# Splitting the scalings of int4 weight granules into parts behind named ScalarE copies

## The chip, the cores and the metric

The program runs on one core of one Trainium2 chip. The profile names the core's engines: PE (TensorE, matmuls; PEld is its weight load), DVE (VectorE), ACT (ScalarE), POOL (GpSimd) and SP (SyncE, which here issues nearly all DMAs). Each engine runs its own instructions in the order in which the program lists them and waits on semaphores for the others. The metric is device time in microseconds, lower is better; the kernel before takes 1338.17 us (median of three runs, 1336.70 to 1338.47).

## The reference

A block of 2048 tokens of width 1024 is normalised; the output is the input plus two branches on the normalised rows: a long convolution along the width with a kernel of a state-space model (S4), and a gated feed-forward layer whose weights are int4 with a scale and a zero for each group of 64.

```python
def dequantize(W_q, scale, zero):
    hi = W_q >> 4 & 15
    lo = W_q & 15
    w = jnp.stack([hi, lo], axis=-1).reshape(out, half * 2)
    w = (w.reshape(out, -1, 64) - zero[:, :, None]) * scale[:, :, None]
    return w.reshape(out, half * 2)
...
xn = layernorm(x)                                  # x: 1 x 2048 x 1024
g = einsum('bsh,ih->bsi', xn, Wg)                  # Wg, Wu: 2752 x 1024
u = einsum('bsh,ih->bsi', xn, Wu)
y = einsum('bsi,hi->bsh', silu(g) * u, Wd)         # Wd: 1024 x 2752
out = x + s4_convolution(xn) + y
```

## The kernel before

**Numbers and products.** Values are kept as pairs of f16 (a high and a low part), and a product takes three matmuls: high by high, high by low, low by high (PASS). Gate and up, and later down, are multiplied by a Strassen-like scheme of seven products in place of eight (PROD, line 63): sums of the token blocks (made by combine, lines 237 to 285) are multiplied by sums of the weight blocks (made by sums, lines 336 to 345).

**Granules.** Weights come in granules of 128 x 1024. j counts 21 column blocks of gate and up; granules 2j and 2j + 1 belong to block j. A granule of gate/up is made so, all in one buffer w:

- load_raw: the raw int4 words and the scales and zeros, two loads issued by SP (lines 292 to 298);
- unpack: two DVE instructions, w <- raw (lines 309, 310);
- scale_c: three small POOL instructions that turn scale and zero into a factor and an offset, sz <- sz (lines 320 to 325);
- w_scale: 16 ACT instructions, one for each group of 64, w <- w,sz (lines 327 to 334);
- w_sums: four DVE instructions, w <- w;
- w_hi: two ACT casts, nat <- w; w_lo: two DVE subtractions, nat <- w,nat; w_t: two transposing DMAs on SP, wf <- nat.

The pools in the gate/up stage: one buffer w, five of "nat" (shared with the down weights' nd and with the work tiles of S4), four raw, two sz, four wf (two blocks' worth). wf of block j + 1 takes the place of block j - 1.

**Order of the stages.** First the 16 norms of 128 rows each (norm_stat, norm_hi, norm_lo: DVE, POOL, ACT, DVE), blocks j = 0 and 1 in plain products (gate_up_plain), combine(0) and combine(1) for the two halves cp of the tokens, and granules 4 to 7. The norms and combines on DVE and ACT are chained in program order (pin). Then the gate/up stage: 38 units gate_up(j, cp), with the down weights (load_wd, four steps a unit from j = 4 on) and the S4 kernel's preparation (s4) as steps between them. Then the convolution, and the down product.

**A unit** (gate_up, lines 595 to 648) is seven products of 12 matmuls. Its ACT work is six instructions: the copy of A to B, of C to hb, of B to D, the Silu of A, and, for the last unit's pending products 4 and 3, the copy of C to ha and the Silu of D. Product 6 adds into B and product 5 into D, so PE needs those two copies.

**What sets the order.** The program is written as a sequence of instructions for each engine by a planner: it takes an instruction when its inputs and its buffer are free by the planner's own time model, and among those that are ready the one that stands first in the text. tc.issue_after(x) adds that what is traced under it and runs on the engine of x stands behind x on that engine; it is a lower bound and no wait. Under heads[behind] all 16 scalings of the granules 2j + 2 and 2j + 3 stand behind the copy of B in unit (j - 1, 1) (lines 384 to 386 and 991 to 994), and their text stands ahead of the units of j. BEHIND = {4: 13} puts the unpack of granule 4 (and, as tiles of one name are handed out in the order of the text, the granules after it) behind the subtraction of norm 13. FETCH traces the loads of granules 8 and 9 under an instruction of POOL; they are SP's, so it moves nothing.

```python
for j in range(2, NJ):
    if 3 <= j < NJ - 1:
        load_w(2 * j + 2, (j - 1, 1))
        load_w(2 * j + 3, (j - 1, 1))
    for cp in range(2):
        if cp or j > 3:
            gate_up(j, cp, wt[j])
```

The last two granules (G_WP, the rest of the down weights) are made after the units of j = 19.

Of the kernel before, what the change touches and what calls it, by code (L numbers as in the profile page):

```python
# [24 lines left out]
F16 = mybir.dt.float16  # L25
# [3 lines left out]
AF = mybir.ActivationFunctionType  # L29
# [4 lines left out]
P = 128  # L34
# [4 lines left out]
NJ = 21  # L39
# [3 lines left out]
G_WP = G_WD + 2 * NPAIR  # L43
# [4 lines left out]

SPG = 8
FETCH = {8: 15, 9: 15}  # L50
BEHIND = {4: 13}

XS = 64.0
WS = 1024.0
# [33 lines left out]
def build(nc, tc, x, xp, raw_d, sz_d, par_d, vct_d, tab_d, csrow_d, out):  # L88
# [3 lines left out]
    with es:  # L92
# [12 lines left out]
        WPN = dr.tile([P, 2, 2048], F16, name="WPN")  # L105
# [8 lines left out]
        V, A = Engine(tc, nc.vector), Engine(tc, nc.scalar)  # L114
        SP, G, PE = Engine(tc, nc.sync), nc.gpsimd, Engine(tc, nc.tensor)
# [22 lines left out]
        def wtemp(kind, shape, dtype, name):  # L138
            return home[kind].tile(shape, dtype, tag=kind, name=name, **({"bufs": szbufs[0]} if kind == "sz" else {}))
# [35 lines left out]
        rs, los = {}, {}  # L175
# [110 lines left out]


        with ea:
            slots, heads, tails, ends = {}, {}, [], [None]
            rawt = {}  # L290

            def load_raw(gi):
                raw = wtemp("raw", [P, 16, 32], I32, f"raw{gi}")
                ld = SP
                ld.dma_start(raw, raw_d[gi].rearrange("p (a b) -> p a b", a=16))
                sz = wtemp("sz", [P, 2, 16], F32, f"sz{gi}")
                ld.dma_start(sz, sz_d[gi])
                return raw, sz
# [21 lines left out]
            def scale_c(gi, sz):  # L320

                G.tensor_scalar(sz[:, 0], sz[:, 0], WS, None, ALU.mult)  # L322
                G.tensor_tensor(sz[:, 1], sz[:, 1], sz[:, 0], ALU.mult)
                G.tensor_scalar(sz[:, 1], sz[:, 1], -1.0, None, ALU.mult)
                return sz

            def scale_a(w, sc, groups=range(16)):

                wv = w.rearrange("p a b -> p (a b)")
                for g in groups:  # L330
                    A.activation(
                        wv[:, 64 * g : 64 * g + 64], wv[:, 64 * g : 64 * g + 64].bitcast(I32), AF.Identity,
                        bias=sc[:, 1, g : g + 1], scale=sc[:, 0, g : g + 1],
                    )
# [30 lines left out]
            def wtile(gi):  # L365
                if gi not in wft:
                    wft[gi] = wfp.tile([P, 28, P], F16, tag="wf", name=f"wf{gi}")
                return wft[gi]
# [9 lines left out]
            made, halved = {}, {}  # L378

            def w_unpack(gi):  # L380
                w, sz = unpack(gi)
                made[gi] = w, scale_c(gi, sz)

            def w_scale(gi, part, behind=None):
                with tc.issue_after(heads[behind].ins) if behind in heads else nullcontext():
                    scale_a(*made[gi], range((0, 5, 11)[part], (5, 11, 16)[part]))

            def w_sums(gi):
                sums(made[gi][0], False)
# [8 lines left out]
            def w_lo(gi):  # L398
                w, _ = made.pop(gi)
                for k, nat in enumerate(halved[gi]):  # L400
                    V.tensor_tensor(nat[:, :, 1], w[:, :, P * k : P * k + P], nat[:, :, 0], ALU.subtract)

            def w_t(gi):
                wf = wtile(gi)
                for k, nat in enumerate(halved.pop(gi)):
                    last[0] = SP.dma_start_transpose(wf[:, 14 * k : 14 * k + 14], nat.rearrange("p a b c -> p (a b c)"))
                wt.setdefault(gi // 2, []).append(wf)

            def load_w(gi, behind=None):
                if gi in BEHIND:  # L410
                    with tc.issue_after(los[BEHIND[gi]].ins):
                        w, sz = unpack(gi)
                    made[gi] = w, scale_c(gi, sz)
                else:
                    w_unpack(gi)
                for part in range(3):
                    w_scale(gi, part, behind)
                w_sums(gi)
                w_hi(gi)
                w_lo(gi)  # L420
                w_t(gi)


            def wp_hi(i):
                made[G_WP + i] = made[G_WP + i][0], wtemp("nat", [P, 1024], F16, f"wph{i}")
                w, hi = made[G_WP + i]
                A.copy(hi, w.rearrange("p a b -> p (a b)")[:, :1024])

            def wp_lo(i):
                w, hi = made.pop(G_WP + i)  # L430
                lo = wtemp("nat", [P, 1024], F16, f"wpl{i}")
                V.tensor_tensor(lo, w.rearrange("p a b -> p (a b)")[:, :1024], hi, ALU.subtract)
                SP.dma_start(WPN[:, i, 0:1024], hi)
                SP.dma_start(WPN[:, i, 1024:2048], lo)

            def scales_t():

# [154 lines left out]

            pending = []

            def gate_up(j, cp, wf):

                def prod(i, ps, start, stop):
                    fa, fb = PROD[i]
                    xt = xtile(cp, fb)
                    for kt in range(4):  # L600
                        for n, (wi, xi) in enumerate(PASS):
                            ends[0] = PE.matmul(
                                ps, wf[kt // 2][:, 14 * (kt % 2) + 2 * fa + wi, :], xt[:, xi, kt, :],
                                start=(start and kt == 0 and n == 0), stop=(stop and kt == 3 and n == 2),
                                skip_group_check=not start,
                            )

                def rest(i):
                    if len(pending) > i:
                        pending[i]()  # L610

                nm = f"{j}_{cp}"
                isc = 1.0 / (XS * WS)
                add, mult = ALU.add, ALU.mult
                bA, bB = bank("A" + nm), bank("B" + nm, "B")
                prod(1, bA, True, True)
                heads[j, cp] = A.copy(bB, bA)
                bC = bank("C" + nm)
                prod(7, bC, True, True)
                tag = "h" if j % 2 else "e"  # L620
                hb = htile("hb_" + nm, tag)
                A.copy(hb, bC)
                rest(0)
                prod(6, bB, False, True)
                bD = bank("D" + nm, "D")
                A.copy(bD, bB)
                rest(1)
                pending.clear()
                prod(2, bA, False, True)
                A.activation(bA, bA, AF.Silu, scale=isc)  # L630
                prod(5, bD, False, True)
                tails.append(V.tensor_tensor(hb, bD, hb, add))

                def fourth():
                    prod(4, bC, False, True)
                    ha = htile("ha_" + nm, tag)
                    A.copy(ha, bC)
                    V.tensor_tensor(ha, bB, ha, add)
                    V.scalar_tensor_tensor(ha, ha, HS * isc, bA, mult, mult)
                    pending[1] = lambda: third(ha)  # L640

                def third(ha):
                    prod(3, bD, False, True)
                    A.activation(bD, bD, AF.Silu, scale=isc)
                    V.scalar_tensor_tensor(hb, hb, HS * isc, bD, mult, mult)
                    finish_h(j, cp, ha, hb)

                pending.extend((fourth, None))
# [283 lines left out]
            wt = {j: [wtile(2 * j), wtile(2 * j + 1)] for j in range(2)}  # L932
# [53 lines left out]
            wd_steps = (None for u in range(NPAIR) for _ in load_wd(u))  # L986
            s4_steps = s4()

            gate_up(2, 0, wt[2])
            gate_up(3, 0, wt[3])  # L990
            for j in range(2, NJ):
                if 3 <= j < NJ - 1:
                    load_w(2 * j + 2, (j - 1, 1))
                    load_w(2 * j + 3, (j - 1, 1))
                for cp in range(2):
                    if cp or j > 3:
                        gate_up(j, cp, wt[j])
                    for _ in range(4 if j >= WD_FROM else 0):
                        next(wd_steps, 0)
                    for _ in range(3 - cp if j >= S4_FROM else 0):  # L1000
                        next(s4_steps, 0)
                if j == NJ - 2:
                    for i in range(2):
                        w_unpack(G_WP + i)
                        for part in range(3):
                            w_scale(G_WP + i, part)
                        wp_hi(i)
                        wp_lo(i)
            settle()
            for steps in (wd_steps, s4_steps):  # L1010
                for _ in steps:
# [163 lines left out]
        for cp in range(2):  # L1175
# [12 lines left out]
            behind = []  # L1188
# [216 lines left out]
```

## Time and profile before

| | us |
|---|---|
| median of three runs | 1338.17 |
| the profiled execution | 1336.8 |
| its span (first to last instruction) | 1335.0 |
| norms, plain products, combine(0) | 0 to about 133 |
| gate/up stage | about 133 to 884 |
| convolution, then the down product | 884 to 1335 |
| PE idle from 133 to 150 | 7.5 |
| PE idle from 150 to 350 | 0.05 |
| PE idle from 350 to 884 | 30.2 |

A line of the timeline gives start, length, engine, source line, operation and, in brackets, how long the engine had been idle and what ended that. L77 is the line in which the helper class records an instruction, L82 the same for those chained by pin, so tiles tell the lines apart: w<-w,sz are scalings, nat<-w the casts of gate/up granules, nd<-w those of the down weights. The granted clock of PE has two values in this profile, full and half.

### The profile page before, as it was taken

The numbers are of one execution on the slowest core, as the hardware profiler recorded it, in microseconds if no ns is written. First come the engines' busy times: TensorE is split into PE (matmuls) and PEld (weight loads), VectorE is DVE, ScalarE is ACT, GpSimd is POOL, SyncE is SP. The second block draws the span as 40 slices with busy tenths as digits, with TensorE's granted clock in tenths as the row PEclk, the third lists the DMA queues.
The fourth block names the chain that finished last, engine by engine and source line by source line (L and its number), as shares of the span: only waits on it lengthen the run. The fifth ranks groups of instructions, "written<-read, shape, count | busy, mean of one in ns | idle before, by whom it ended". The sixth has DMA issues, their size and how long they took to land. (4 is left out here: it accounts for less than half of the span.)

```text
span 1335.0 us, 20888 instructions
## 1 busy us (share of the span) xinstructions
PE 1277.1 (96%) x7880; PEld 751.0 (56%) x7880; DVE 991.1 (74%) x1344; ACT 669.1 (50%) x1208; POOL 189.7 (14%) x267
## 2 busy tenths in 40 slices
PE   6999799999999989989989999999999999999998
PEld 5644344444444434434433444456557888888887
DVE  7759986568797787779668687662738897779792
ACT  4777457647664745557466756720204433443330
POOL 3220010100000100111001001000000022255540
PEclk8999899999999998999999999999999999999999
DMA  6792947459896988699789979695937779799991
GB/s 224 181 189 52 218 137 137 124 142 234 193 257 160 236 204 226 156 226 239 185 222 226 242 191 223 201 281 183 329 132 296 259 201 270 241 260 265 288 189 50
DMA packets 358400, 276.02 MB, mean 207 GB/s; under 512 B 211668, under 2 KB 304668, under 8 KB 354204
## 3 DMA queue, kind: packets, MB, share of 16 engines
q1 hardware_dynamic: 335676, 261.59, 71.4%
q0 software_dynamic: 21760, 10.49, 6.6%
q10 hardware_dynamic: 864, 2.62, 0.6%
q8 instruction: 61, 1.00, 0.3%
q14 instruction: 39, 0.32, 0.1%
HBM read 132.36 MB, written 94.84 MB: 170 GB/s over the span
## 5 line engine op out<-in xcount | busy, mean ns | idle before, releaser
L77 PEld LDWEIGHTS <-wf 128*128 128x128 f16 x3960 | 374.1, 99 | 473.7 <-issue 40.6
L77 PEld LDWEIGHTS <-g 128*128 128x128 f16 x2940 | 287.6, 98 | 33.5 <-issue 0.2
L77 ACT ACTIVATE w<-w,sz 128x64 f32<-128x64 int32 x640 | 217.1, 426 | 64.1 <-DVE w L77 54.4
L77 PE MATMUL A<-x,wf 128*128 128x512 f16 x912 | 216.7, 384 | 13.9 <-DMA wf<-nat 13.1
L77 PE MATMUL D<-x,wf 128*128 128x512 f16 x912 | 214.3, 382 | 10.3 <-ACT D L77 9.7
L77 PE MATMUL C<-x,wf 128*128 128x512 f16 x912 | 210.2, 381 | 1.2 <-ACT hb L77 1.2
L77 DVE TENSOR_TENSOR w<-w 128x256 f32<-128x256 f32 (+2 forms) x272 | 139.0, 527 | 77.6 <-ACT w L77 71.3
L77 ACT CAST g<-a 128x2560 f16<-128x2560 f32 x42 | 97.5, 2324 | 180.8 <-PE cv L77 51.2
L77 PE MATMUL A<-b,g 128*128 128x256 f16 x1680 | 185.9, 273 | 0.0
L77 DVE TENSOR_TENSOR g<-a,g 128x2560 f16<-128x2560 f32 x42 | 118.3, 2819 | 30.9 <-ACT g L77 30.9
L1257 POOL DMA_DIRECT2D out<-o x64 | 78.7, 2105 | 342.7 <-DVE o L77 334.2
L322 POOL TENSOR_SCALAR sz<-sz 128x16 f32<-128x16 f32 x42 | 29.6, 705 | 685.3 <-DMA sz<-in_sz 588.5
L77 PE MATMUL B<-x,wf 128*128 128x512 f16 x456 | 108.1, 388 | 9.6 <-ACT B L77 9.5
L77 ACT CAST nd<-w 128x896 f16<-128x896 f32 x70 | 63.5, 933 | 67.0 <-DVE w L77 56.0
L77 PE MATMUL D<-b,g 128*128 128x256 f16 x840 | 94.0, 273 | 0.0
L77 ACT CAST nat<-w 128x896 f16<-128x896 f32 x76 | 68.1, 936 | 46.0 <-issue 31.2
L77 DVE TENSOR_TENSOR nd<-w,nd 128x896 f16<-128x896 f32 x70 | 75.2, 1082 | 21.4 <-ACT nd L77 21.3
L77 DVE TENSOR_TENSOR nat<-w,nat 128x896 f16<-128x896 f32 x76 | 80.2, 1085 | 13.9 <-ACT nat L77 13.8
L77 PEld LDWEIGHTS <-x 128*128 128x128 f16 x576 | 52.4, 98 | 23.8 <-issue 2.7
L77 DVE SCALAR_TENSOR_TENSOR p<-cv,p 128x512 f32<-128x512 f32 x32 | 21.9, 686 | 49.5 <-PE cv L77 47.7
L77 PE MATMUL cv<-band,x 128*128 128x512 f16 (+3 forms) x384 | 57.0, 299 | 0.0
L77 PE MATMUL g<-x,wf 128*128 128x128 f16 (+1 forms) x336 | 48.5, 292 | 1.5 <-ACT wf L82 0.8
(145 smaller groups left out, 1199.6 us busy)
## 6 DMA issues: line engine op xcount, KB each, us to landing
a<-HF SPq DMA_DIRECT2D x28, 1280.0 KB, 8.0
WD<-nd SPq DMA_DIRECT2D x70, 448.0 KB, 4.2
b<-WD SPq DMA_DIRECT2D x49, 640.0 KB, 6.0
w<-SZT SPq DMA_DIRECT2D x80, 256.0 KB, 5.5
raw<-in_raw SPq DMA_DIRECT2D x65, 256.0 KB, 3.5
HF<-ha SPq DMA_DIRECT2D x54, 256.0 KB, 3.3
HF<-s SPq DMA_DIRECT2D x40, 256.0 KB, 3.5
HF<-hb SPq DMA_DIRECT2D x36, 256.0 KB, 3.1
```

The costliest lines, as they stand in the source:

```text
L77: return method(*args, **kw)
L322: G.tensor_scalar(sz[:, 0], sz[:, 0], WS, None, ALU.mult)
L1257: G.dma_start(dst, o[:, q], accum_op=ALU.add)
```

## The change

- The granules from 8 on, and the two of G_WP, are made by one generator, w_flow, that the units drive. It does one granule in a unit's time: behind the copy of B to D 8 scalings; behind the Silu of A the other 8, then the loads of the next granule are traced and the sums; behind the next unit's copy of A to B the two casts, and then the subtractions, the transposes and the unpack of the next granule. The ties are again issue_after, so lower bounds.
- The flow begins in the second unit (3, 0). Granule g is scaled in unit number g - 7 (the first unit is 0) and cast at the head of the next one.
- The text of the parts stands right behind the copy that they are tied to, no longer ahead of both units of j.
- Granule 4's unpack stands behind the subtraction of norm 15 instead of 13, and its three POOL instructions behind POOL's last one of norm 15.
- wp_hi and wp_lo do the same as before with another index.

```diff
-BEHIND = {4: 13}
+BEHIND = {4: 15}
...
-            def w_scale(gi, part, behind=None):
-                with tc.issue_after(heads[behind].ins) if behind in heads else nullcontext():
-                    scale_a(*made[gi], range((0, 5, 11)[part], (5, 11, 16)[part]))
+            def w_scale(gi, groups=range(16)):
+                scale_a(*made[gi], groups)
...
-            def load_w(gi, behind=None):
+            def load_w(gi):
                 if gi in BEHIND:
                     with tc.issue_after(los[BEHIND[gi]].ins):
                         w, sz = unpack(gi)
-                    made[gi] = w, scale_c(gi, sz)
+                    with tc.issue_after(rs[15, 0].ins):
+                        made[gi] = w, scale_c(gi, sz)
...
+            def w_flow():
+                order = list(range(8, 2 * NJ)) + [G_WP, G_WP + 1]
+                for n, gi in enumerate(order):
+                    w_unpack(gi)
+                    for groups in (range(8), range(8, 16)):
+                        mark = yield
+                        with tc.issue_after(mark.ins):
+                            w_scale(gi, groups)
+                    if n + 1 < len(order):
+                        rawt[order[n + 1]] = load_raw(order[n + 1])
+                    if gi < G_WP:
+                        w_sums(gi)
+                    mark = yield
+                    with tc.issue_after(mark.ins):
+                        (w_hi if gi < G_WP else wp_hi)(gi)
+                    if gi < G_WP:
+                        w_lo(gi)
+                        w_t(gi)
+                    else:
+                        wp_lo(gi)
+                while True:
+                    yield
...
-                heads[j, cp] = A.copy(bB, bA)
+                seed = A.copy(bB, bA)
+                if len(started) > 1:
+                    side.send(seed)
...
-                A.copy(bD, bB)
+                seed = A.copy(bD, bB)
+                if len(started) == 1:
+                    next(side)
+                if started:
+                    side.send(seed)
...
-                A.activation(bA, bA, AF.Silu, scale=isc)
+                seed = A.activation(bA, bA, AF.Silu, scale=isc)
+                if started:
+                    side.send(seed)
+                started.append((j, cp))
...
-                if 3 <= j < NJ - 1:
-                    load_w(2 * j + 2, (j - 1, 1))
-                    load_w(2 * j + 3, (j - 1, 1))
...
-                if j == NJ - 2:
-                    for i in range(2):
-                        w_unpack(G_WP + i)
-                        for part in range(3):
-                            w_scale(G_WP + i, part)
-                        wp_hi(i)
-                        wp_lo(i)
```

## The prediction

> **What bounds the kernel now.** I read the page first, then the windows by stage, the waits of TensorE (PE) inside the gate/up stage, and the timeline at its longest idle times. The page's first line and the group of scalings:
>
> ```profile
> PE 1277.1 (96%) x7880; PEld 751.0 (56%) x7880; DVE 991.1 (74%) x1344; ACT 669.1 (50%) x1208; POOL 189.7 (14%) x267
> ...
> L77 ACT ACTIVATE w<-w,sz 128x64 f32<-128x64 int32 x640 | 217.1, 426 | 64.1 <-DVE w L77 54.4
> ```
>
> PE is busy for 96% of the span: all the change can win is PE idle time and half-clock time. By windows:
>
> ```profile
> 133.00:150.00 17.00, 9.46 (x24) 2.43 (x23) 16.97 (x23) 9.65 (x17) 0.00 (x0) 0.70 1.09 196
> 150.00:350.00 200.00, 199.95 (x938) 91.16 (x937) 141.34 (x228) 118.83 (x259) 14.32 (x36) 1.00 0.69 167
> ```
>
> (Columns: window, length, busy time and count of PE, PEld, DVE, ACT, POOL, granted clock, DMA share, GB/s.) PE starves at 133-150, where DVE has no idle time left; it never waits at 150-350; the rest of its waits lie at 350-884. Waits of PE from 133 to 884 us (engine and tile waited for, us in total, times, longest):
>
> ```profile
> PE A L77 <- DMA wf<-nat: 13.1, 12, 3.3
> PE D L77 <- ACT D L77: 9.7, 7, 4.1
> PE B L77 <- ACT B L77: 9.5, 4, 3.4
> ```
>
> One of the waits for a ScalarE (ACT) copy, in the timeline of all engines:
>
> ```profile
> 672.26 5.41 ACT L77 ACTIVATE w<-w,sz 128x64 f32<-128x64 int32 x16 [2.91 <-DVE w L77]
> ...
> 677.57 0.57 ACT L77 COPY B<-A 128x512 f32<-128x512 f32 x1
> ...
> 678.20 1.02 PE L77 MATMUL B<-x,wf 128*128 128x512 f16 x4 [3.42 <-ACT B L77]
> ```
>
> All 16 scalings of a granule stand as one block before the copy of A to B, and PE waits 3.42 us for it.
>
> **Part 1: half bursts behind named copies.** A block of 16 takes 5.41 us (0.34 each). One unit is 84 matmuls of 0.216 us, 18.1 us. Between the end of product 1 and the start of product 6, which needs the copy of B, lie products 7 and the last unit's 4: 2 x 12 x 0.216 = 5.2 us, less the copy's 0.57: 4.6 us of slack. D's copy has the same slack before product 5. A block of 5.41 exceeds it; the new half of 8 (2.7 us) doesn't, nor do the two casts (1.78 us). And a half stands right behind D's copy or the Silu of A, so the next urgent copy is a product or more away. Gaps that I put to a 16-block in the ACT timeline: 0.69 us (at 358), 1.24 + 0.58 (562), 2.82 (578), 3.42 (678), 2.71 (794), 0.56 (840): 12.0 us. Two of them were followed by a half-clock stretch of 3.4 us, 1.7 us lost each. Together 15.4. The bounds: 0 if all are replaced, 15.4 if all go; I take **-12**, near the upper end, since the slack covers the halves but other ACT work (casts for the down weights, 0.93 us each) still comes between.
>
> The clock is weighed here. Rows: after PE idled 2.71 us at 794.69, twelve matmuls took 4.44 us instead of 2.75; after 2.82 us at 578.66 they took 2.75. The Trainium skill (TensorE: Matmul & The Clock Gate, section "Why this matters for your kernels") asks for no PE-idle gaps over some 3 us; by it the 2.71 us gap would have cost no clock and the upper end would be 13.7, not 15.4. The rows decide: a gap just under 3 us can cost clock.
>
> **Part 2: odd granules earlier.** PE waits for turned weights (wf) at 482-730: 1.00, 0.92, 0.99, 0.76, 0.73, 0.64, 0.52, together 5.6 us. All are a unit's first product waiting for the second granule of its pair, whose casts started 1.6 to 11.3 us after the B copy of the unit before (at 563.8 against 552.5, for one). They are now traced behind that copy. Worked out from a unit's start: B copy ends at 3.2, casts at 5.0, landing 7 to 8 us later (casts ended 721.4, landed 729.6): 13.2 us, against 18.1 when it is needed, 4.9 us spare. The sums before the casts (4 x 0.42 on DVE) wait for the second half behind Silu A: 15.6 + 0.6 + 2.7 = 18.9, so 20.6, which is 2.5 us into the next unit, before the B copy. Bounds: -5.6 (all gone) to +5 (the new order is late by 0.3 us in each of 17 iterations); I take **-3**.
>
> **Part 3: granule 4 behind the last norm.** In the timeline at 87-104:
>
> ```profile
> 87.69 5.41 ACT L77 ACTIVATE w<-w,sz 128x64 f32<-128x64 int32 x16
> ...
> 94.93 1.23 ACT L82 ACTIVATE n<-n,rs 128x1024 f32<-128x1024 f32 x1
> ...
> 96.06 4.07 ACT L77 ACTIVATE w<-w,sz 128x64 f32<-128x64 int32 x12
> ...
> 100.80 1.05 ACT L82 CAST n<-n 128x1024 f16<-128x1024 f32 x1
> ...
> 101.87 1.22 DVE L82 TENSOR_TENSOR n<-n 128x1024 f16<-128x1024 f32 x1 [0.38 <-ACT n L82]
> ```
>
> The scalings of granules 4 and 5 stand before the last norm (its Pool step ended at 90.33). DVE idles 2.52 + 0.90 + 3.59 + 0.88 + 0.38 = 8.3 us there, and every later step of combine(0) stands behind the row at 101.87. With granule 4's unpack behind that row, ACT does 1.23 + 1.05 after 90.33 and the row starts near 92.7, 9.2 us earlier; DVE is saturated afterwards, so combine(0) ends up to 8.3 us sooner. At 133-150 PE did 24 matmuls, 5.2 us of work in 17: 11.8 lost. What is late next: the second operand of product 7, from combine(0)'s end, and granule 5's halves. The latter's transposes were issued at 134.8 though they were ready at 124.4, because SP stood behind a store at 126.1-130.9; 8 us of delay there costs nothing. Bounds: +2 (the weights become the last) to -8.3; I take **-6**, near the DVE rows. Pool's three instructions for granule 4 (0.26, 1.10, 0.25 at 30.6-32.4) now stand behind norm 15's, done by 91.9, before the unpack ends: 0. The Pool wait at 64.6-69.5 is for granule 7's scales, which the change doesn't tie: 0.
>
> **Part 4: everything that moves along.** Per granule: a raw and a scale load (SP, 0.38 and 0.33 us issue), two unpacks on DVE (0.42), three Pool steps, 16 scalings, 4 sums, 2 casts, 2 subtractions (1.08), 2 transposes on SP. Counts stay. Granule 9's loads are traced twice (once as prefetch, once by FETCH): 272 KB, some 0.7 us of SP, at 190-210 where PE doesn't wait: 0; without that cover 3.5 us, the landing time of a raw load. The halves now wait for the unpack right behind D's copy; behind them on ACT stand the Silu of the last unit's D and of A, for which only products on DVE and a bank needed a unit later wait: 0. The casts behind the B copy are different: if one waits for a "nat" buffer, the copies hb, ha and D stand behind it, and PE waits for D. That happened before:
>
> ```profile
> 498.17 1.78 ACT L77 CAST nd<-w 128x896 f16<-128x896 f32 x2 [9.11 <-issue]
> ...
> 502.00 0.59 ACT L77 COPY D<-B 128x512 f32<-128x512 f32 x1
> ...
> 502.64 1.01 PE L77 MATMUL D<-x,wf 128*128 128x512 f16 x2 [4.11 <-ACT D L77]
> ```
>
> Gaps of this kind: 0.42, 1.36, 0.77, 4.11, 0.58, 1.77 = 9.0 us, and 2.9 of half clock after 4.11: 12 us, 2.0 each. No buffer is added, and an even granule's pair is held longer (casts 3 us into a unit, but its wf slot is free only after the pending product 3, 13 us into it). Bounds: -6 (half of them go, since the copies stand first) to +56 (34 units at 2.0, less the 12 there are); I take **+2**, nearest to the six rows.
>
> **Sum.** The profiled execution took 1336.8 us (span 1335.0 and 1.8 around it): 1336.8 - 12 - 3 - 6 + 2 = 1317.8. The median of the three runs, 1338.17, is 1.4 above it: **1319 us**.
>
> **Rivals.**
> 1. *Only the blocks go or only the norms move*: the order is laid out by a planner on its own estimates, so one of parts 1 and 3 may not take effect (the norms' cast may be put behind other ACT work; the blocks may join again, since a tie is only a lower bound). 1338.2 - 6 to -12 with the +2 kept and part 2 gone: about 1328 to 1334. For: ACT waits 51.9 us for DVE before scalings, so halves may bunch. Against: the D copy now stands between.
> 2. *Slower, by nat buffers*: casts right behind each B copy meet full buffers. Price 2.0 us per unit; it cancels the 21 us of parts 1 to 3 from 10 to 11 units on. In 24 of 34 units: 1338.2 + 48 - 12 - 21 = 1353. For: five buffers, two held 15 us or more per even granule, and the s4 tables take up to three. Against: 150-350 shows no PE wait at the same pace.
> 3. *All goes well*: 15.4 + 5.6 + 8.3 + 6 = 35 us less: 1303.
>
> **Chances.** Forecast (1308 to 1327) 0.42, rival 1 (1328 to 1341) 0.22, rival 2 0.24, rival 3 0.12. A measurement here can tell 0.2% (2.7 us) from no change. Faster 0.67 (forecast, rival 3 and 0.13 of rival 1), same 0.08, slower 0.25 (the rest of rival 1 and rival 2). The range 1303 to 1350 leaves out 0.19: the far part of rival 2 (0.14) and 0.05 of rival 3. The likeliest case's own range is 1308 to 1327.
>
> **What would show it.** Right: no block of 16 scalings on ACT in the gate/up stage; waits of PE for ACT's B copies near 0 instead of 9.5 us; the last norm's subtraction near 93 instead of 101.87; PE idle at 133-150 under 3 us. Wrong: ACT casts "nat" waiting several us behind a B copy with "PE D <- ACT D" growing; new PE waits for wf at unit starts; granule 4's weights landing after 140.

## The result, and the profile after

The changed kernel takes 1343.68 us (median of six runs, 1341.27 to 1347.04) against 1336.88 us (six runs, 1332.38 to 1338.47) for the kernel before: a ratio of 1.0062, 95% interval 1.0049 to 1.0075. It is slower by 0.6%, where the forecast said 1319 us and faster. The profiled execution took 1347.04 us, the longest of the six, and its span is 1343.6.

The same views as for the kernel before, now of the changed one. The page: the sum of PE's work is nearly the same, and a group that had waited for little now has 53.4 us of idle time of VectorE before it (columns: busy us, mean ns, idle before and what ended most of it).

```profile
PE 1280.8 (95%) x7880; PEld 751.1 (56%) x7880; DVE 992.1 (74%) x1344; ACT 671.1 (50%) x1208; POOL 188.2 (14%) x267
...
L77 DVE TENSOR_TENSOR w<-raw,w 128x1024 f32<-128x1024 int16 x20 | 24.4, 1220 | 53.4 <-DMA raw<-qn 53.4
```

The windows, the last one the whole gate/up stage (133 to 884 before, where PE was busy for 713.22 of 751 us):

```profile
133.00:150.00 17.00, 12.06 (x48) 4.30 (x47) 16.91 (x24) 10.45 (x23) 0.00 (x0) 0.90 1.03 183
150.00:350.00 200.00, 197.41 (x923) 89.05 (x922) 135.41 (x222) 116.74 (x258) 13.55 (x34) 1.00 0.70 169
133.00:893.00 760.00, 717.26 (x3279) 318.49 (x3278) 562.48 (x922) 452.36 (x975) 57.70 (x108) 0.98 0.83 199
```

PE did 48 matmuls in 133 to 150 where it had done 24, but the stage ends 10 us later. PE's waits from 133 to 893 us:

```profile
PE A L77 <- DMA wf<-nat: 33.7, 25, 3.2
PE D L77 <- DVE hb L77: 3.1, 2, 2.0
PE B L77 <- ACT B L77: 2.2, 2, 1.6
PE C L77 <- DVE ha L77: 1.4, 1, 1.4
PE D L77 <- ACT D L77: 1.3, 2, 1.0
```

The waits for ScalarE's copies of B and D fell from 19.2 us to 3.5, as meant. In their place PE waits for turned weights: 28.8 of the 33.7 us lie after 160 us, at the first product of units (j, 0), where the kernel before had 5.6. The half-clock time from 150 to 900 us also rose, from 17.1 to 23.9 us; from 133 us on it is 27.3 us in both, since the kernel before had 10.2 us of it in the first 17 us.

Where it was lost: I compared the time at which PE reaches the matmuls of the n-th unit in both traces. The changed kernel is 3.1 us ahead half a unit in and 0.8 at unit 4, 0.7 behind at unit 13, 10.2 behind at unit 16, then between 1.3 and 10.8 behind, and 10.1 at the end of the stage. After the stage the difference no longer grows: the two profiled executions differ by 10.2 us (the medians by 6.8).

Two stretches of the timeline show how a granule comes late. First, the odd granule 17 in the changed kernel. The copy that its casts are tied to started at 348.12, and its four sums had ended by 351.2:

```profile
354.24 0.94 ACT L77 CAST nd<-w 128x896 f16<-128x896 f32 x1 [3.50 <-DVE w L77]
...
358.04 0.94 ACT L77 CAST nd<-w 128x896 f16<-128x896 f32 x1 [2.38 <-DVE w L77]
358.88 1.77 ACT L77 CAST nat<-w 128x896 f16<-128x896 f32 x2
...
361.19 5.07 SPq L77 DMA_TRANSPOSE wf<-nat  x2
...
363.03 1.09 DVE L77 TENSOR_TENSOR nat<-w,nat 128x896 f16<-128x896 f32 x1
...
366.55 0.82 PE L77 MATMUL A<-x,wf 128*128 128x512 f16 x3 [1.98 <-DMA wf<-nat]
```

The casts (nat) were ready at 351.2 and ran at 358.88, because two casts for the down weights (nd) stood ahead of them in ScalarE's order and those waited for VectorE. The second subtraction, the second transpose and PE followed late in turn. Second, granule 19:

```profile
396.74 1.26 SPq L77 DMA_TRANSPOSE raw<-qn  x1
...
403.87 1.23 DVE L77 TENSOR_TENSOR w<-raw,w 128x1024 f32<-128x1024 int16 x1 [4.97 <-DMA raw<-qn]
...
406.12 1.78 ACT L77 CAST nat<-w 128x896 f16<-128x896 f32 x2 [6.44 <-DVE w L77]
...
408.82 3.70 SPq L77 DMA_TRANSPOSE wf<-nat  x2
...
412.98 0.82 PE L77 MATMUL A<-x,wf 128*128 128x512 f16 x3 [1.98 <-DMA wf<-nat]
```

Here VectorE itself stands: at the first instruction of a down granule's dequantisation, for a transpose of its raw words that was issued late. The last sums of granule 19 and the rest stand behind it. VectorE's waits, of the changed kernel from 150 to 900 us and then of the kernel before from 150 to 884:

```profile
DVE w L77 <- DMA raw<-qn: 53.4, 10, 9.0
```

```profile
DVE w L77 <- DMA w<-SZT: 29.2, 14, 5.7
```

So VectorE stood there before too, for the table of scales (SZT) instead. Two causes were left to tell apart, VectorE's stand and the place of the casts, and beside them the early load of raw words and the ties themselves.

### The profile page after: what moved, and what is told of

Its sections match the earlier page's. It is cut to its first block, busy times and chain, and to the rows that moved or that the text cites. A ratio compares the mean times of both kernels' runs of the same rounds, so it can differ in the third digit from the quotient of the medians.

```text
span 1343.6 us, 20880 instructions
## 1 busy us (share of the span) xinstructions
PE 1280.8 (95%) x7880; PEld 751.1 (56%) x7880; DVE 992.1 (74%) x1344; ACT 671.1 (50%) x1208; POOL 188.2 (14%) x267
## 5 line engine op out<-in xcount | busy, mean ns | idle before, releaser
L77 PE MATMUL A<-x,wf 128*128 128x512 f16 x912 | 217.8, 384 | 33.9 <-DMA wf<-nat 33.7
L77 PE MATMUL C<-x,wf 128*128 128x512 f16 x912 | 216.5, 388 | 2.0 <-DVE ha L77 1.4
L77 DVE TENSOR_TENSOR g<-a,g 128x2560 f16<-128x2560 f32 x42 | 118.3, 2819 | 30.9 <-ACT g L77 30.9
L322 POOL TENSOR_SCALAR sz<-sz 128x16 f32<-128x16 f32 x42 | 23.0, 547 | 697.7 <-DMA sz<-in_sz 601.3
L77 PE MATMUL B<-x,wf 128*128 128x512 f16 x456 | 104.9, 379 | 2.4 <-ACT B L77 2.2
L77 ACT CAST nat<-w 128x896 f16<-128x896 f32 x76 | 67.8, 935 | 36.4 <-DVE w L77 11.7
L77 DVE TENSOR_TENSOR nd<-w,nd 128x896 f16<-128x896 f32 x70 | 75.5, 1086 | 12.6 <-ACT nd L77 12.4
L77 DVE TENSOR_TENSOR w<-raw,w 128x1024 f32<-128x1024 int16 x20 | 24.4, 1220 | 53.4 <-DMA raw<-qn 53.4
```

Source lines behind the costliest of these rows:

```text
L77: return method(*args, **kw)
```

## The experiments

Each ran on one chip beside the kernel before, which took 1336.02 to 1336.62 us (medians) there, and its ratio is to those runs. Theories P and T stand in the expectations from the fifth experiment on; "theory P" is that the flow's places in the program make the granules late.

**1. Without the early load.** The flow traces the next granule's loads ahead of the sums; could that push the down pair's loads back?

```diff
-                    if n + 1 < len(order):
-                        rawt[order[n + 1]] = load_raw(order[n + 1])
```

> The changed kernel without the early load of the next granule: its raw words are traced in its own unpack, as before. Theory A (raw buffers): the early load holds one of the four raw buffers through a unit, the down weights' unpack (qn) must wait for one, its transposes land late, DVE stands 53.4 us at the first dequantisation of each pair, and the granules' sums and subtractions queued behind it make wf late. Then DVE's waits for raw<-qn fall under 10 us, PE's waits for wf after 160 us fall from 28.8 to under 12 us, ScalarE copies stay cheap (under 6 us), and the time falls from 1343.7 to 1320-1332. Theory B (the ties): the casts stand a unit too late because they are tied behind the next unit's B copy. Then the waits for wf stay near 29 us and the time at 1341-1346.

1356.31 us, ratio 1.0154 (1.0137 to 1.0171): worse by 12.6 us than the changed kernel. The wait for raw<-qn is gone from VectorE's list, but the one for w<-SZT is back at 51.3 us, 14 times. The early load isn't the cause of the stand: without it VectorE stands at the same place for another transfer. The time lies outside both ranges. PE's waits for wf fell only to 24.4 us, those for hb rose from 3.1 to 10.6 and those for the copies of B and D from 3.5 to 8.3; why they rose stays open.

**2. The norms' part alone**, on the kernel before.

```diff
-BEHIND = {4: 13}
+BEHIND = {4: 15}
...
-                    made[gi] = w, scale_c(gi, sz)
+                    with tc.issue_after(rs[15, 0].ins):
+                        made[gi] = w, scale_c(gi, sz)
```

> The kernel before with granule 4 behind norm 15 on DVE and POOL, and nothing else. The prediction gave -6 us for it. In the changed profile the last norm's subtraction ran at 93.8 instead of 101.9, but the first product began at 136.6 instead of 135.1 and four units on the gain was 0.8 us. Both theories: 1333-1337 (0 to -3 us against 1336.9). If the prediction's step holds after all: 1329-1332.

1336.96 us, ratio 1.0007 (0.9995 to 1.0019): no difference. PE is 2.8 to 3.0 us ahead at units 1 to 3, 0.1 to 0.6 behind at units 4 to 11 and 1.4 behind at the end of the stage.

**3. The flow alone**: the changed kernel with the three edits of the second experiment taken back.

> The changed kernel with granule 4 behind norm 13 as before, and its scale steps untied: the flow of parts alone. Both theories put the loss into the flow: 1342-1349, with PE's waits for wf after 160 us at 25-32 us and DVE's waits for raw<-qn at 45-60 us. If the loss came from the norms' part instead: at or under 1337.

1347.53 us, ratio 1.0087 (1.0067 to 1.0107); PE waits 27.2 us for wf after 160 us (28.8 in the changed kernel), VectorE 51.8 us for raw<-qn. The loss belongs to the flow.

**4. The second dequantisation later.** On the changed kernel, the second granule of a down pair is dequantised behind the last sum (hb) of the unit before, as the first one was already.

```diff
                 mb = ready_wd.pop(gb)
-                dequant(*mb)
+                with tc.issue_after(tails[-1].ins):
+                    dequant(*mb)
```

> The changed kernel, early loads kept, with the second dequantisation of a pair of down granules tied behind the newest tail on DVE, so that DVE no longer meets it before its transposes have landed. Theory A: the DVE waits for raw<-qn fall from 53 to under 20 us, the waits for wf to 10-20 us, the time to 1328-1338. Theory B: no change in the waits for wf, 1341-1347.

1338.27 us, ratio 1.0016 (1.0002 to 1.0030), 5.4 us below the changed kernel. VectorE's wait for raw<-qn is nearly gone (2.0 us), but PE still waits for wf (the first two lines of its list, 150 to 900 us):

```profile
PE A L77 <- DMA wf<-nat: 19.7, 12, 4.5
PE B L77 <- ACT B L77: 10.2, 4, 5.0
```

The time lies just above theory A's 1328 to 1338. VectorE's stand is one cause and not the only one.

**5. Without the ties.** The parts of the flow at the same places of the program, none tied to a copy.

```diff
-                        with tc.issue_after(mark.ins):
-                            w_scale(gi, groups)
+                        w_scale(gi, groups)
...
-                    with tc.issue_after(mark.ins):
-                        (w_hi if gi < G_WP else wp_hi)(gi)
+                    (w_hi if gi < G_WP else wp_hi)(gi)
```

> Leaves out the ties alone: the flow gives the same parts at the same places of the text, but no scaling and no hi cast waits for a named copy. Theory T (the hi cast's tie to the first copy of the next unit makes the odd granule of each pair late): the product A's waits for wf after 160 us, 28.8 us in the changed kernel, fall to 6 to 14 us, the product's waits for the copies B and D rise from some 4 towards 19 us, and the time comes to 1334 to 1342 us. Theory P (a granule for each unit, at these places of the text, is late whatever its ties): wf waits stay at 24 us or more, and with the copies late again on top the time is 1348 to 1358 us.

1351.4 us, ratio 1.010 (1.008 to 1.012). PE's waits for wf are 24.4 us, a little less than with the ties. The odd granules' casts start on average 6.4 us after the copy of B in unit (j - 1, 1), against 6.1 with the ties (worked out from ScalarE's instructions, 16 pairs). On average the tie holds nothing back; theory T in its narrow form, that the tie makes the granule late, falls, and the time lies in theory P's range. The waits for the copies of B and D rise from 3.5 us to 11.4, still below the 19.2 of the kernel before: of that gain about half is the ties', the rest comes with the places in the program.

**6. Every part one copy earlier**: the first half of the scalings behind the copy of B, the second behind the copy of D, the casts behind the Silu. In the program the casts now stand ahead of the down steps that follow each unit, not behind them.

```diff
-                if len(started) > 1:
-                    side.send(seed)
+                if len(started) == 1:
+                    next(side)
+                if started:
+                    side.send(seed)
                 bC = bank("C" + nm)
...
                 seed = A.copy(bD, bB)
-                if len(started) == 1:
-                    next(side)
                 if started:
```

> Every part of the flow is given one copy earlier: first half of the scalings behind the first copy of a unit, second half behind the second, hi casts behind the Silu of the same unit instead of the first copy of the next. One granule for each unit as before. Theory T (the last tie comes too late): the odd granule is ready some 5 to 7 us sooner, the product A's waits for wf after 160 us fall from 28.8 to below 14 us, time 1330 to 1337 us. Theory P (work queued ahead of the casts on VectorE and ScalarE makes them late, not the tie): wf waits stay above 22 us, time 1341 to 1346 us.

1339.59 us, ratio 1.003 (1.0017 to 1.0042). PE's waits and, in the second fence, VectorE's, 150 to 900 us:

```profile
PE B L77 <- ACT B L77: 23.7, 10, 5.4
...
PE A L77 <- DMA wf<-nat: 1.9, 3, 1.0
```

```profile
DVE w L77 <- DMA w<-SZT: 66.9, 16, 12.7
```

The waits for wf fell from 28.8 us to 1.9: the place decides. The odd casts now start 3.3 us before the copy of B of (j - 1, 1) on average. But the time is 1339.59, above the 1330 to 1337 that went with that, since another wait took over: now VectorE stands longer and buffers stay full, so the casts run late, and since they stand ahead of the copy, they hold it up. ScalarE's casts for gate/up waited 71.4 us for VectorE's sums (11.7 in the changed kernel) and 52.8 at "issue" (7.4). Of the nine longest waits for the copy of B, 23.5 us, 10.6 us follow a cast that waited at "issue", 6.5 one that waited for VectorE's sums, and 6.4 one that waited for a store of down weights (WD<-nd) to free its buffer. One of the first kind:

```profile
363.81 1.78 ACT L77 CAST nat<-w 128x896 f16<-128x896 f32 x2 [6.43 <-issue]
365.50 1.98 ACT L77 CAST nd<-w 128x896 f16<-128x896 f32 x2
...
367.38 0.58 ACT L77 COPY B<-A 128x512 f32<-128x512 f32 x1
...
368.01 2.75 PE L77 MATMUL B<-x,wf 128*128 128x512 f16 x12 [1.66 <-ACT B L77]
```

"issue" names nothing that the profile shows; that it is a full nat buffer is what I infer from the order of the work. In part this is the second rival of the prediction, in another place.

**7. The kernel before with the second dequantisation later**: the edit of experiment 4 on the kernel of experiment 2.

> The granules' order of the kernel before, with scales of granule 4 behind norm 15, and the second dequantisation of a down pair held behind the end of the last unit's sum, as in the run of that edit on the changed kernel. If VectorE standing at the dequantisations (29.2 us of waits for the scales' table in the kernel before) delays granules there too: 1330 to 1334 us. If that stand is covered in the old order (its wf waits after 160 us are only 5.6 us): 1335 to 1339 us, no change.

1318.22 us, ratio 0.9866 (0.9848 to 0.9883). I had put 1330 to 1334 as the better case; it is 18.7 us below the kernel of experiment 2 (1336.96). The stand was not covered in the old order. PE, VectorE:

```profile
PE B L77 <- ACT B L77: 9.7, 4, 4.3
PE A L77 <- DMA wf<-nat: 5.5, 6, 2.6
...
PE D L77 <- ACT D L77: 1.5, 2, 0.8
```

```profile
DVE w L77 <- DMA w<-SZT: 8.6, 3, 4.9
```

Against experiment 2, VectorE's wait for the table went from 31.1 us to 8.6, ScalarE's casts for gate/up waited 13.4 us at "issue" in place of 30.9, and PE's waits for D's copy went from 10.2 to 1.5.

**8. Both: a copy earlier, and the second dequantisation later**, on the changed kernel.

> Both edits on the changed kernel: every part one copy earlier, and the second dequantisation behind the end of the last unit's sum. Theory T: the two gains add, wf waits after 160 us below 10 us, time 1325 to 1332 us, below both kernels. Theory P: 1335 to 1341 us, as the second edit alone.

1312.69 us, ratio 0.9816 (0.9798 to 0.9833). Below both kernels, and more than the two edits alone: 4.1 us (experiment 6) and 5.4 (experiment 4) make 9.5 on the changed kernel, together they bring 31.0. Each had left the other's wait in place. PE's waits, 150 to 900 us:

```profile
PE D L77 <- DVE hb L77: 12.1, 5, 3.8
PE B L77 <- ACT B L77: 1.9, 2, 1.6
...
PE A L77 <- DMA wf<-nat: 1.4, 3, 0.6
PE D L77 <- ACT D L77: 0.9, 2, 0.5
```

What is late next is VectorE with its own queue of work: a sum (hb) that frees the bank of D comes up to 3.8 us late. In three of the five waits, 8.2 of the 12.1 us, steps of the S4 preparation (s4n) stand close ahead of it, and VectorE isn't idle just before it in any.

**9 to 11. Three parts of the change on the kernel of experiment 8.** The ties off (the diff of experiment 5), the norms' part off (that of experiment 2 reversed), the early load off (that of experiment 1).

> The run with every part one copy earlier and the second dequantisation held back, with the ties of scalings and hi casts to named copies taken off; the places in the program stay. Theory 'place' (what counts is that the hi casts stand in the program ahead of the unit's four down steps; the tie itself holds nothing): 1310 to 1317 us, as with ties. Theory 'tie' (as in the forecast's Part 1: without ties the 16 scalings stand in front of the copies B and D, 19 us in the kernel before, and halves mend it): waits for the copies B and D rise from 2.8 to 12 us or more, 1321 to 1332 us.

> The same run without the third part of the change: granule 4's unpacking behind norm 13 again and its scales free. Theory 'given back' (the first stage's gain is lost by unit 4 whatever follows, as in the run of that part alone): within 2 us of 1312.7, 1310 to 1315 us. Theory 'covered' (the gain was only hidden by the later stalls for wf, which are gone here): 1315.5 to 1321 us, 3 us or more above.

> The same run without the early load of the next granule's raw weights. On the changed kernel leaving it out cost 12.6 us, through VectorE standing at the table of the down pair's scales. Theory 'order of the table's load' (the early load keeps SP's loads ahead of the table's): 1320 to 1328 us, with waits for the table back above 40 us. Theory 'only the second dequantisation' (held back it no longer meets the table): 1310 to 1316 us.

| kernel | us | ratio (interval) |
|---|---|---|
| experiment 8 | 1312.69 | 0.9816 (0.9798 to 0.9833) |
| without the ties | 1320.68 | 0.9878 (0.9858 to 0.9898) |
| without the norms' part | 1315.45 | 0.9847 (0.9832 to 0.9863) |
| without the early load | 1310.98 | 0.9813 (0.9798 to 0.9829) |

The ties are worth 8.0 us once the weights come in time: without them ScalarE has 26 unbroken blocks of 16 scalings or more after 150 us, with them 3, and PE waits 9.2 us for the copy of B instead of 1.9:

```profile
PE B L77 <- ACT B L77: 9.2, 4, 2.7
PE D L77 <- DVE hb L77: 6.0, 4, 3.2
```

The time lies just under the 1321 us, and the waits for the copies (9.2 + 1.5 us) just under the 12 us, that went with theory "tie"; theory "place", 1310 to 1317, falls. The norms' part may be worth up to 2.8 us here; the intervals just touch, and 1315.45 lies between the two ranges, so it stays open. In the profiled executions (1314.89 and 1314.05 us) the kernel without it is 6.2 us behind half a unit in, 0.5 from unit 23 on and 0.8 at the end of the stage: most of the gain is given back there too, only later. The early load makes no difference: once the second dequantisation is held back, it no longer meets the table.

## Why the prediction was wrong, step by step

- **What bounds the kernel** was right for PE: the time follows PE's idle time in the gate/up stage. I read only PE's waits, though. VectorE's 29.2 us of waits for w<-SZT were in the profile before, and I took them for the waits of an engine that isn't the bottleneck. Experiment 7 shows that moving the instruction that stood there is worth 18.7 us.
- **Part 1 (-12)** held. The copies of B and D cost PE 3.5 us instead of 19.2, which takes in the six gaps that part 4 had put to casts waiting for buffers. One sign of being right didn't come, "no block of 16 scalings": the halves rejoined in 17 granules of the changed kernel (counted in ScalarE's order), yet few of those blocks met a copy that PE needed. By experiments 8 and 9 the ties are worth 8.0 us.
- **Part 2 (-3) is the step that failed**, with the wrong sign and beyond its bound of +5. "Worked out from a unit's start: B copy ends at 3.2, casts at 5.0" takes ScalarE as free behind the copy it is tied to, and the "7 to 8 us" from there to the landing are one row's. A tie is a lower bound, and behind the copy stood what the program lists ahead of the casts: the casts for the down weights of the four steps between two units, which wait for VectorE. Against the copy of B in (j - 1, 1) the odd casts came 2.4 us later on average before (-13.3 to 11.4), and 6.1 after (0.5 to 12.6); from the cast to the second transpose it was 4.7 us and is 7.3. The spare time that I had worked out was 4.9 us. The old order had the text of both granules ahead of the units of j, and so ahead of those steps. I had checked the copies that stand behind the casts, and not the casts that stand ahead of them. PE's waits for wf after 160 us went up by 23.2 us.

  Late casts are only a part of it. The units of j = 7 to 11, 13 and 17, whose odd casts came 7.2 to 12.6 us after the copy, hold 12.6 of the 28.8 us (at j = 14 and 20 casts as late cost nothing). Another 14.6 us lie at j = 12, 15, 16, 18 and 19, where the casts came 1.0 to 3.0 us after it, and the steps behind them were late. At j = 12 and 18 (5.6 us) the subtractions stood behind VectorE's waits of 7.59 and 9.01 us for raw<-qn. At j = 15, 16 and 19 (9.0 us) the subtractions had ended 4.6 to 5.4 us after the copy, but SP issued the transposes only 6.8 to 11.2 us after it, behind other DMAs in its order. For j = 19, whose copy started at 801.47:

```profile
802.47 1.77 ACT L77 CAST nat<-w 128x896 f16<-128x896 f32 x2
...
804.23 2.08 DVE L77 TENSOR_TENSOR nat<-w,nat 128x896 f16<-128x896 f32 x2
...
806.37 2.07 SPq L77 DMA_DIRECT2D WD<-nd  x2
...
809.54 0.34 SPq L77 DMA_DIRECT2D raw<-in_raw  x1
...
809.98 4.20 SPq L77 DMA_TRANSPOSE wf<-nat  x2
...
814.56 0.82 PE L77 MATMUL A<-x,wf 128*128 128x512 f16 x3 [2.38 <-DMA wf<-nat]
```

  So the sum lacked the queues of three engines, not of ScalarE alone.
- **Part 3 (-6)** came true in its first steps and brought nothing on the kernel before (experiment 2). The last norm's subtraction starts at 93.82 (92.7 forecast, 101.87 before), with no scalings between the norms:

```profile
90.86 1.24 ACT L82 ACTIVATE n<-n,rs 128x1024 f32<-128x1024 f32 x1 [0.79 <-POOL rs L187]
92.74 1.04 ACT L82 CAST n<-n 128x1024 f16<-128x1024 f32 x1
93.82 1.23 DVE L82 TENSOR_TENSOR n<-n 128x1024 f16<-128x1024 f32 x1 [0.37 <-ACT n L82]
```

  The last step of combine(0) ends 8.4 us sooner (137.07 against 145.44), but the transposes of granule 4 are issued at 132.37 instead of 130.95, SP again standing behind a store, and PE's first product starts at 136.6 instead of 135.1. The weights are the last to come, the "+2" end of the bounds at first. PE idles 4.9 us from 133 to 150 instead of 7.5; the forecast's sign was under 3. PE is then 3.1 us ahead and has lost all but 0.8 of it by unit 4. The traces show it waiting for wf again on the way: 0.72 us at 162.87 and 0.78 at 212.68 in the changed kernel, 2.46 at 212.94 in experiment 2, where the kernel before has no wait. The weights of the next blocks come no sooner, so a lead isn't kept.
- **Part 4 (+2)**: the cost by way of D's copy didn't come in the changed kernel (PE waited 1.3 us for it instead of 9.7). Full buffers did: ScalarE's casts waited 25.1 us for stores of down weights (WD<-nd), which free the nat buffers, and 7.4 at "issue"; before it was 2.3 and 42.1 us. They now make casts late (by 3.9 us at j = 13) and no longer D's copy. In experiment 6, where the casts stood ahead of the copy, it was the copy of B that they held up. The traced order of the down pair was no part of my sum; the new wait for raw<-qn, 53.4 us of VectorE, cost 5.4 us (experiment 4).
- **The sum by measured terms**: part 2's term is +23.2 us where the forecast had -3; put in its place it makes 1345 of the forecast's 1319, so part 2 alone turns the sign. PE's waits from 133 us on do not add up to the whole: -15.7 (copies) + 23.2 (wf) - 2.6 (wf before 160 us, 7.5 to 4.9) + 2.6 (hb) - 2.8 (s4n, 2.8 to 0) = +4.7, and 1336.8 + 4.7 = 1341.5 for the profiled execution, which took 1347.04. By the two traces the stage's first product comes 1.5 us later and its end 10.1: PE idles 41.7 us in between instead of 36.2, and its 3269 matmuls take 715.2 us instead of 712.1. Of these 3.1 us 0.9 is work at half clock (25.9 us instead of 24.1); some 2 us stay open.
- **The rivals**: none named this. "Slower, by nat buffers" had the right side with the wrong mechanism in the main: its cost ran through D's copy. The prediction's list of signs did hold "new PE waits for wf at unit starts", which is what came.

Left open: whether the S4 steps alone make hb late in experiment 8, what the norms' part is worth there, why experiment 1 is slower than the changed kernel, and those 2 us.

## What to carry to other kernels

A tie to a named instruction says only what work stands behind; when it runs is set by everything that the program lists ahead of it on that engine, so go through that list, with what each entry waits for, before giving a time to a moved step, and do the same for the engines that take the result on: here VectorE's and SP's queues cost about as much as ScalarE's. An engine that isn't the bottleneck but stands still in the middle of its queue holds up all that is queued behind it: its waits are worth a look wherever it feeds the bottleneck, and here moving one such instruction brought the kernel of experiment 2, which is as fast as the kernel before, 18.7 us. When a fix only swaps one wait for another, try it together with the fix of the second wait: two edits worth 9.5 us apart brought 31.0 together.

## What the runs showed of the hardware that I had not expected

PE's clock fell to half after idle gaps shorter than 3 us, and the length of a gap didn't decide it. In the changed kernel a lone gap of 1.98 us (ended at 412.98) was followed by 3.4 us at half clock, and another of 1.98 us (366.55) and one of 1.90 (491.30) were not; 2.00 and 1.71 us, ended at 531.20 and 533.74, were, like 2.12 and 1.51 us, ended at 576.05 and 578.60.

What fits is where the gaps lie. In both traces the stretches of half clock between 150 and 900 us begin whole multiples of 3.41 us apart (414.15, 451.70, 533.62 and so on). I divided the gate/up stage from 150 us on into windows of that length on that grid. In the two kernels together, all ten windows at full clock in which PE idled 1.97 us or more were followed by half clock, and none with 1.80 us or less; of three in between, one (1.84) was and two (1.90 and 1.92) were not. So the idle time in such a window counts, whether it is one gap or two. That also tells apart the two rows of the prediction: the gap of 2.71 us that ended at 794.69 lay in one window, and the grid splits that of 2.82 (578.66) into 0.90 and 1.92.

Windows of the changed kernel and what followed them (length, PE's busy time; the granted clock is the third number from the right):

```profile
489.18:492.59 3.41, 1.51 (x8) 0.60 (x7) 3.18 (x6) 2.83 (x7) 0.00 (x0) 1.00 1.03 230
491.00:495.00 4.00, 3.70 (x18) 1.69 (x19) 3.77 (x9) 4.00 (x13) 0.00 (x0) 1.00 1.04 260
410.74:414.15 3.41, 1.43 (x8) 0.59 (x7) 3.34 (x7) 2.87 (x9) 0.00 (x0) 1.00 1.14 210
414.15:417.56 3.41, 3.41 (x10) 1.23 (x9) 3.19 (x8) 3.05 (x10) 0.00 (x0) 0.50 0.50 170
530.21:533.62 3.41, 0.82 (x3) 0.21 (x3) 3.31 (x16) 3.18 (x9) 0.00 (x0) 1.00 1.15 230
533.60:537.00 3.40, 3.26 (x8) 1.19 (x9) 3.26 (x8) 3.40 (x11) 0.00 (x0) 0.50 0.81 298
```

A weight that comes in two transposes makes a pair of gaps: PE waits for the first half, does three or four matmuls, and waits for the second. The Trainium skill (TensorE: Matmul & The Clock Gate, section "Why this matters for your kernels") asks for no PE-idle gaps over some 3 us; these runs show that a gap of 2 us, or two shorter ones close together, can cost clock too.
